# Keys and queries of a decoder layer's cross-attention by seven block products, with the context's keys from memory and two batches routed at a time

## The chip, the cores and the metric

The kernel runs on one core of a Trainium2 chip. The metric is the device time of one execution in microseconds, the median of the runs. All arithmetic is in 32-bit floats.

## The reference

Sixteen batches of 256 tokens of width 256 (`x`) pass a post-norm decoder layer of three parts; each batch has a context of 77 rows of width 256.

```python
x = layernorm(x + recurrence(x))
x = layernorm(x + cross_attention(ctx, x))
x = layernorm(x + experts(x))

# cross_attention, 8 heads of 128; xn, ln: normed context and tokens, with gains and biases
q = ln @ Wq + bq
kv_input = concatenate([xn, ln], axis=1)          # 77 + 256 rows
k, v = split(kv_input @ Wkv + bkv, 2)
attn = softmax((q * DH**-0.5) @ k.T)              # each head: 256 x 333
out = (attn @ v) @ Wo + bo

# experts: each token to its 2 best of 8 (512 wide), each expert takes its first 512 tokens
```

The recurrence is a projection to 512, a convolution over four tokens, silu, and a scan over the tokens with 16 states. What counts here is `k` and `q`: both are products of the same 256 tokens, K from 333 rows (the tokens and the context), Q from the 256 tokens alone.

## The kernel before, in words

**Stages.** A start loads weights and prepares batch 0. Then 128 heads (16 batches of 8) run one after the other, and between them, by a table written out by hand, the pieces of all other work: the recurrence of later batches, the preparation of the next batch's keys and values, the projection, norm, scoring and routing of the batch before. A stage for the experts follows.

**A head.** `head_kq` (L581) makes K of a head in two products with 333 moving columns (L587; 256 tokens and 77 context rows, `kvt`) and Q in two with 256 (L592); ACT moves both out of the accumulator with bias and scale (L589, L594). `head_softmax` makes the scores (L602) in one two-bank tile, DVE takes the row maximum (L604), ACT the exponentials with their sums (L608), DVE the reciprocal and the normed rows `pn` (L610, L613). `head_turn` transposes these on TensorE (L625); DVE copies the first 512 columns (`ptt`, L627) and ACT the 77 rows of the context (L628). `head_out` multiplies with the values (L639) and ACT moves the result out (L647). The loop (from L1263) interleaves three heads:

```python
        if i < len(heads):
            head_kq(*heads[i])
            for f, args in steps[heads[i]]:
                f(*args)
        if i >= 2:
            head_out(*heads[i - 2])
        if i < len(heads):
            head_softmax(*heads[i])
        if 1 <= i <= len(heads):
            turned = head_turn(*heads[i - 1])
        if i < len(heads):
            for f, args in late_steps[heads[i]]:
                f(*args)
```

`steps` and `late_steps` are the table: `at(b, h, ...)` puts a piece ahead of a head's output product, `behind(b, h, ...)` after the turn. A scheduler lays the instructions out on each engine's queue near this order; each queue then runs in order, SyncE's (SP) DMA queue too.

**Seven products.** Values and projection already use the scheme by which a product of two-by-two blocks takes seven block products in place of eight, with sums of blocks: `prep_values` (L541) with `tsum` (sums of token blocks, `prep_sums`, L530, on GpSimd) and `wsum`; `project_pairs` (L711, its products at L729) with 128-column products that each have their own weights. Keys and queries do not use it.

**Context.** `context_turn` (L431) turns the normed context into `kvc`, an SBUF tile for all batches; `context` (L454) makes the context's values once and stores them in memory (`vc`), from where each batch loads its rows (L549). The context's keys are computed again in every head, as 77 of the 333 columns.

**Routing.** `choose` (L838) finds each token's two experts by some sixteen small DVE operations on 128x16, `dispatch` (L880) counts places by two small products (L886, L887), computes the rows by some twenty more small DVE operations and scatters the tokens by four indirect DMAs of GpSimd (L921). Both run for each batch. What later stages must know of a token lies in six columns behind its 256 (`DX = D + 6`).

**Recurrence.** `rec_in` (L315) is a piece of projection and convolution: four passes of 512 columns on TensorE (L324), two ACT operations (L333, L342) and five DVE operations (L337, L339 three times, L344). `rec_state` (L348) ends with a product `pp` (L385) that waits for DVE's `zb`, and the scan.

Of the kernel before, what the change touches and what calls it, by code (L numbers as in the profile page):

```python
# [10 lines left out]
F32 = mybir.dt.float32  # L11
I32 = mybir.dt.int32
# [26 lines left out]
def decoder_layer(  # L39
# [40 lines left out]
    xpool = ctx.enter_context(tc.tile_pool(name="x", bufs=5))  # L80
# [11 lines left out]

    vc_d = dram.tile([B * M, INNER], F32, tag="vc", name="vc")
# [10 lines left out]
    rev = cpool.tile([P, GT, E], F32, tag="rev", name="rev")  # L104
    ebase = cpool.tile([P, GT, E], F32, tag="ebase", name="ebase")
# [79 lines left out]
    wosum = wpool.tile([P, 3, H // 2, P], F32, tag="wosum", name="wosum")  # L185
    wsum = wpool.tile([P, 4, 512], F32, tag="wsum", name="wsum")

    kvc = wpool.tile([P, DC, B * M], F32, tag="kvc", name="kvc")
# [40 lines left out]
    ctx_ends = [b2.tile([P, 1, D], F32, tag="ctx", name=f"ctx{t}") for t in (0, NCT - 1)]  # L229
# [55 lines left out]
    V.tensor_scalar(bqs, bq_s, DH**-0.5, None, ALU.mult)  # L285

# [61 lines left out]
    def rec_state(first, last):  # L348
# [34 lines left out]
        A.activation(dec[R], dec[R], AF.Exp, scale=-1.0)  # L383
        pp = bank(f"pp{first}")
        T.matmul(pp[R, 0:S], lhsT=perm[R, R], rhs=zb[R], start=True, stop=True)  # L385
        bs = aw.tile([P, S], F32, tag="bs", name=f"bs{first}")
# [42 lines left out]
    turns = {}  # L429

    def context_turn(t, first):  # L431
# [11 lines left out]
        for k in range(DC):  # L443
            T.transpose(pt[:, k * P : k * P + rows], zc[0:rows, 0, k * P : (k + 1) * P], ident[0:rows, 0:rows])
        for k in range(DC):
            A.activation(
                kvc[:, k, t * P : t * P + rows],
                pt[:, k * P : k * P + rows],
                AF.Identity,
                bias=bm[:, k : k + 1],  # L450
                scale=gm[:, k : k + 1],
            )

    def context(t, first):  # L454
# [4 lines left out]
        for half in range(2):  # L459
# [9 lines left out]
            for k in range(DC):  # L469
                T.matmul(  # L470
                    pv[0:rows],
                    lhsT=kvc[:, k, t * P : t * P + rows],
# [10 lines left out]
        if first:  # L483
            nc.sync.dma_start(vc_d[t * P : t * P + rows, :], stages[t // 2][0:rows, t % 2, :])

# [17 lines left out]
    def prep_keys(b):  # L503

        zl = zs.pop(b)
        kvt = b2.tile([P, DC, J], F32, tag="kvt", name=f"kvt{b}")
        G.tensor_copy(kvt[:, :, S:J], kvc[:, :, b * M : (b + 1) * M])
# [22 lines left out]
    def prep_sums(b):  # L530

        x = lambda i, k: kvts[b][:, k, i * P : (i + 1) * P]
        sums = b1.tile([P, 4, P], F32, tag="tsum", name=f"tsum{b}")
# [47 lines left out]
    def head_kq(b, h):  # L581

        kvt = kvts[b]
        f = slice(h * DH, (h + 1) * DH)
        pk = bank(f"pk{b}_{h}", "pk", 1)
        for k in range(DC):
            T.matmul(pk[:, 0:J], lhsT=wkv_s[:, k, f], rhs=kvt[:, k, :], start=(k == 0), stop=(k == DC - 1))  # L587
        kt = b2.tile([P, J], F32, tag="kt", name=f"kt{b}_{h}")
        A.activation(kt, pk[:, 0:J], AF.Identity, bias=bkv_s[:, h : h + 1])  # L589
        pq = bank(f"pq{b}_{h}", "pq", 1)  # L590
        for k in range(DC):
            T.matmul(pq[:, 0:S], lhsT=wq_s[:, k, f], rhs=kvt[:, k, 0:S], start=(k == 0), stop=(k == DC - 1))  # L592
        qt = b2.tile([P, S], F32, tag="qt", name=f"qt{b}_{h}")
        A.activation(qt, pq[:, 0:S], AF.Identity, bias=bqs[:, h : h + 1], scale=DH**-0.5)  # L594
        kts[b, h], qts[b, h] = kt, qt

    def head_softmax(b, h):
# [7 lines left out]
        p = b2.tile([P, 2, J], F32, tag="p", name=f"p{b}_{h}")  # L605
# [5 lines left out]
        pn = b2.tile([P, 2, J], F32, tag="pn", name=f"pn{b}_{h}")  # L611
        for ic in range(2):
            V.tensor_scalar(pn[:, ic, :], p[:, ic, :], rs[:, ic : ic + 1], None, ALU.mult)  # L613
        pns[b, h] = pn

    def head_turn(b, h):
# [10 lines left out]
        turned = V.tensor_copy(ptt[:, 0:2, :], pt01.rearrange("p (j i) -> p j i", j=2))  # L627
        A.copy(ptt[0:M, 2, :], pt2[0:M, 0:S])  # L628
        ptts[b, h] = ptt
        return turned  # L630
# [18 lines left out]
    pws, norms, xbs = {}, {}, {}  # L649
# [104 lines left out]
    def norm_half(b, i):  # L754

        if i == 0:
            xbs[b] = b1.tile([P, 2, D], F32, tag="xb", name=f"xb{b}")
# [4 lines left out]
        y = b2.tile([P, D], F32, tag="yl", name=f"yl{b}_{i}")  # L762
# [18 lines left out]
    def settle_now(b):  # L781
        r2 = again(*norms.pop(b), f"o{b}")
        o = b1.tile([P, 2, D], F32, tag="yb", name=f"o{b}")
# [29 lines left out]
    def score_experts(b):  # L813
# [12 lines left out]
        lgs[b] = small.tile([P, GT, E], F32, tag="lg", bufs=2, name=f"lg{b}")  # L826
        V.tensor_copy(lgs[b].rearrange("p t e -> p (t e)"), pl[:, 0 : GT * E])

    def t3(tag, b):
        return small.tile([P, GT, E], F32, tag=tag, bufs=2, name=f"{tag}_{b}")  # L830

    def t2(tag, b):
        return small.tile([P, GT], F32, tag=tag, bufs=2, name=f"{tag}_{b}")

    def wide(t):
        return t.unsqueeze(2).broadcast_to([P, GT, E])

    def choose(b):  # L838


        def first_max(src, k, km):
# [6 lines left out]
            V.tensor_tensor(key, eq, rev, ALU.mult)  # L848
            V.tensor_reduce(km, key, AX.X, ALU.max)
            oh = t3(f"oh{k}", b)  # L850
            V.tensor_tensor(oh, key, km.unsqueeze(2).broadcast_to([P, GT, E]), ALU.is_equal)
# [3 lines left out]
        x = xs[b]  # L855
        wa, wb, km1 = x[:, :, D], x[:, :, D + 1], x[:, :, D + 3]
        for i in range(GT):
            G.tensor_scalar(x[:, i, D + 2 : D + 3], tok1, float(b * S + i * P), 1.0, ALU.add, ALU.mult)
        lg = lgs.pop(b)
# [18 lines left out]
        chosen[b] = oh1, oh2m, on  # L878

    def dispatch(b):  # L880

        oh1, oh2m, on = chosen.pop(b)

        pc = bank(f"pc{b}")
        onf = on.rearrange("p t e -> p (t e)")
# [480 lines left out]
```

## Time and profile before

| | before |
|---|---|
| median of 3 runs, us | 1165.93 (1164.40 to 1166.26) |
| the profiled execution: its time, its span, us | 1174.61, 1172.9 |
| busy, us: PE, weight loads, DVE | 1140.7, 833.5, 812.1 |
| busy, us: ACT, GpSimd | 494.5, 321.2 |
| K products (L587), Q products (L592), scores (L602), us | 165.3, 131.2, 164.3 |
| row maximum (L604), turn's copy on DVE (L627), us | 108.3, 87.2 |
| granted TensorE clock | 0.998 |

PE is TensorE, DVE VectorE, ACT ScalarE, POOL GpSimd, SP SyncE. "Busy" is the union of an engine's instructions; those of PE are pipelined, so a row's length is more than its share of the time. A group's row gives busy time, the mean of one in ns, and the idle time of the engine ahead of it with what ended most of it. A row of the waits view is the waiting instruction, what it waited for, total us, times, and the longest.

### The profile page before, as it was taken

How to read it: one execution, taken by the hardware profiler on the slowest of the kernel's cores; microseconds unless marked ns; L12 is line 12 of the kernel's file. 1: busy time of each engine (PE TensorE's matmuls, PEld its weight loads, DVE VectorE, ACT ScalarE, POOL GpSimd, SP SyncE). 2: the span in 40 equal slices, each digit the busy share in tenths (PEclk: the TensorE clock that was granted, in tenths of full speed). 3: DMA queues.
4: the chain of work that ended last, by engine and by line, in shares of the span. 5: the costliest groups of instructions: out<-in, count | busy, mean ns of one | idle time of the engine just before them, and what ended most of it. 6: DMA issues, size and time to landing. Idle time of an engine off the chain costs nothing. (4 is left out here: it accounts for less than half of the span.)

```text
span 1172.9 us, 16419 instructions
## 1 busy us (share of the span) xinstructions
PE 1140.7 (97%) x5436; PEld 833.5 (71%) x5436; DVE 812.1 (69%) x2367; ACT 494.5 (42%) x1298; POOL 321.2 (27%) x564
## 2 busy tenths in 40 slices
PE   7999999999999999999999999999999999999996
PEld 3465676777787877677777777687877778876664
DVE  6655878686757776876678767766576664665665
ACT  3344444443444444444445444444444443523331
POOL 2211243113311331232213322232122212144454
PEclk9999999999999999999999999999999999999999
DMA  7740101001000010000000100000001000045752
GB/s 253 217 144 33 35 22 37 12 28 39 24 25 17 28 37 22 27 29 19 15 10 24 37 14 10 14 19 14 10 14 46 24 10 12 21 162 137 180 161 87
DMA packets 47149, 60.67 MB, mean 52 GB/s; under 512 B 7941, under 2 KB 37102, under 8 KB 47064
## 3 DMA queue, kind: packets, MB, share of 16 engines
q1 hardware_dynamic: 39686, 50.31, 13.5%
q0 software_dynamic: 6048, 9.22, 3.1%
q8 instruction: 43, 0.70, 0.3%
q14 instruction: 42, 0.34, 0.1%
q10 hardware_dynamic: 1330, 0.10, 0.1%
HBM read 36.33 MB, written 30.78 MB: 57 GB/s over the span
## 5 line engine op out<-in xcount | busy, mean ns | idle before, releaser
L639 PE MATMUL po<-ptt,v 128*128 128x256 f32 (+1 forms) x768 | 190.9, 382 | 1.6 <-DVE rs L610 1.6
L639 PEld LDWEIGHTS po<-ptt,v 128*128 128x128 f32 (+1 forms) x768 | 141.5, 190 | 53.1 <-issue 35.5
L587 PE MATMUL pk<-kvt,wkv_s 128*128 128x333 f32 x512 | 165.3, 444 | 0.0
L602 PE MATMUL s<-kt,qt 128*128 128x333 f32 x512 | 164.3, 442 | 0.0
L604 DVE TENSOR_REDUCE nm<-s 128x2 f32<-128x666 f32 x128 | 108.3, 846 | 54.3 <-PE s L602 54.1
L608 ACT ACTIVATE p<-s,nm 128x333 f32<-128x333 f32 x256 | 135.4, 535 | 22.6 <-DVE nm L604 21.9
L647 ACT ACTIVATE ot<-po,bkv_s 128x256 f32<-128x256 f32 x128 | 60.8, 475 | 172.0 <-PE po L639 171.0
L592 PE MATMUL pq<-kvt,wq_s 128*128 128x256 f32 x512 | 131.2, 379 | 0.0
L587 PEld LDWEIGHTS pk<-kvt,wkv_s 128*128 128x128 f32 x512 | 91.1, 191 | 45.9 <-issue 23.2
L602 PEld LDWEIGHTS s<-kt,qt 128*128 128x128 f32 x512 | 96.5, 189 | 30.9 <-issue 0.5
L592 PEld LDWEIGHTS pq<-kvt,wq_s 128*128 128x128 f32 x512 | 96.7, 189 | 30.5 <-issue 0.5
L628 ACT COPY ptt<-pb 77x256 f32<-77x256 f32 x128 | 47.2, 369 | 163.1 <-PE pb L625 163.1
L613 DVE TENSOR_SCALAR pn<-p,rs 128x333 f32<-128x333 f32 x256 | 100.8, 429 | 3.3
L921 POOL DMA_INDIRECT xg<-xs,sidx x64 | 65.6, 1025 | 89.2 <-DVE sidx L918 58.5
L627 DVE COPY ptt<-pa 128x512 f32<-128x512 f32 x128 | 87.2, 682 | 0.6 <-PE pa L625 0.6
L625 PEld LDWEIGHTS pa<-ident,pn 128*128 128x128 f32 x512 | 63.9, 141 | 29.3
L589 ACT ACTIVATE kt<-pk,bkv_s 128x333 f32<-128x333 f32 x128 | 68.9, 538 | 24.6 <-PE pk L587 23.8
L625 PE MATMUL pa<-ident,pn 128*128 128x128 f32 x512 | 76.8, 273 | 0.0
L339 DVE SCALAR_TENSOR_TENSOR cv<-hp,cw,cv 128x512 f32<-128x512 f32 (+1 forms) x108 | 73.9, 691 | 1.4
L594 ACT ACTIVATE qt<-pq,bqs 128x256 f32<-128x256 f32 x128 | 61.0, 477 | 18.8 <-PE pq L592 14.9
L324 PE MATMUL ph<-xT,inw 128*128 128x512 f32 (+1 forms) x144 | 63.4, 570 | 5.0 <-DMA inw<-in_in_wT 4.9
L1183 PE MATMUL pf<-w,it 128*128 128x256 f32 x272 | 61.3, 381 | 2.7 <-ACT ye L1193 1.5
(254 smaller groups left out, 1826.8 us busy)
## 6 DMA issues: line engine op xcount, KB each, us to landing
v<-vc SPq DMA_DIRECT2D x16, 308.0 KB
xg<-zero SPq DMA_DIRECT2D x34, 131.0 KB
xe<-xg SPq DMA_DIRECT2D x8, 524.0 KB
xt<-in_x_in SPq DMA_DIRECT2D x16, 256.0 KB
out<-o SPq DMA_DIRECT2D x16, 256.0 KB
w<-in_w1T SPq DMA_DIRECT2D x8, 512.0 KB
w<-in_w2T SPq DMA_DIRECT2D x8, 512.0 KB
oe<-ye SPq DMA_DIRECT2D x15, 256.0 KB
```

Of the source, the lines that this page charges most:

```text
L339: V.scalar_tensor_tensor(cv, hp[:, :, k : k + S], cw[:, c, k : k + 1], cv, ALU.mult, ALU.add)
L587: T.matmul(pk[:, 0:J], lhsT=wkv_s[:, k, f], rhs=kvt[:, k, :], start=(k == 0), stop=(k == DC - 1))
L589: A.activation(kt, pk[:, 0:J], AF.Identity, bias=bkv_s[:, h : h + 1])
L592: T.matmul(pq[:, 0:S], lhsT=wq_s[:, k, f], rhs=kvt[:, k, 0:S], start=(k == 0), stop=(k == DC - 1))
L602: T.matmul(s[:, ic, 0:J], lhsT=qt[:, ic * P : (ic + 1) * P], rhs=kt, start=True, stop=True)
L604: V.tensor_reduce(nm, s[:, :, 0:J], AX.X, ALU.max, negate=True)
L608: A.activation(p[:, ic, :], s[:, ic, 0:J], AF.Exp, bias=nm[:, ic : ic + 1], accum_out=sm[:, ic : ic + 1])
L613: V.tensor_scalar(pn[:, ic, :], p[:, ic, :], rs[:, ic : ic + 1], None, ALU.mult)
L625: T.transpose(dst[0:jn, c0 : c0 + P], pn[:, ic, j0 : j0 + jn], ident)
L627: turned = V.tensor_copy(ptt[:, 0:2, :], pt01.rearrange("p (j i) -> p j i", j=2))
L639: T.matmul(po[:, 0:S], lhsT=vs[b][0:jn, jc, h * DH : (h + 1) * DH], rhs=ptt[0:jn, jc, :], start=(jc == 0), stop=(jc == 2),)
L921: dma = G.indirect_dma_start(out=xg[:, :], out_offset=bass.IndirectOffsetOnAxis(ap=sidx[:, t, c : c + 1], axis=0), in_=xs[b][:, t, :], in_ ...
```

## The change

Keys and queries of a head become one product of two-by-two blocks (token halves by channel halves; K and Q side by side), in seven 128-column products in one bank, `kq_first` three and `kq_second` four; the sums of the tokens are the ones that the values already use. Their combination is one ACT copy, one ACT operation and five DVE operations of 128 columns. Batch 0 still uses plain products, with the context's columns left out, since its weight sums (`kq_weights`, DVE) are made during it, partly in the place of `wq_s`; so the scale of the queries is put into the weights ahead (`scale_queries`, ACT). The context's keys are computed once (`context_keys`), stored in memory (`kc`), and loaded by a DMA in each head. The products of a head are issued one head ahead. The normed rows are written in place; the turn's copy of 512 columns goes from DVE to ACT. `rec_state` is cut before `pp`: `rec_scan` runs behind the output product. `choose` and `dispatch` run once for two batches (on 128x32, eight scatters in a row, with an ACT copy of the six columns ahead), except for the last two batches. Pools are re-cut to make room.

```diff
+    def scale_queries():
+        A.activation(wq_s..., wq_s..., AF.Copy, scale=DH**-0.5)
...
+    def context_keys(t, first):
+        rows = ctx_rows(t)
...
+            for h in range(4):
+                f = half * 512 + h * DH
+                for k in range(DC):
+                    T.matmul(
+                        pk[:, h, 0:rows],
+                        lhsT=wkv_s[:, k, f : f + DH],
+                        rhs=kvcs[t][:, k, 0:rows],
...
+            bias = bkv_s[:, heads].unsqueeze(2).broadcast_to([P, 4, rows])
+            V.tensor_tensor(kc[:, :, 0:rows], pk[:, :, 0:rows], bias, ALU.add)
+            nc.sync.dma_start(kc_d[:, heads, t * P : t * P + rows], kc[:, :, 0:rows])
...
+    def kq_weights(h):
+        f = slice(h * DH, (h + 1) * DH)
+        t = lambda i: kqsum[:, i, h - BLOCKS[0], :]
+        V.tensor_tensor(t(0), wq_s[:, 0, f], wkv_s[:, 0, f], ALU.subtract)
+        V.tensor_tensor(wq_s[:, 0, f], wq_s[:, 1, f], wq_s[:, 0, f], ALU.subtract)
+        V.tensor_tensor(t(1), wq_s[:, 1, f], t(0), ALU.subtract)
+        V.tensor_tensor(t(2), wkv_s[:, 1, f], t(1), ALU.subtract)
...
+    def kq_first(b, h):
...
+        nc.sync.dma_start(kt[:, S:J], kc_d[:, h, b * M : (b + 1) * M])
...
+        kq_product(b, h, ((0, 1), (1, 5), (2, 7)), True)
+        parts_kq[b, h] = u = b2.tile([P, 3, P], F32, tag="ukq", bufs=1, name=f"ukq{b}_{h}")
+        A.copy(u.rearrange("p r d -> p (r d)"), pk[:, 0 : 3 * P])
+        V.scalar_tensor_tensor(u[:, 1, :], u[:, 1, :], bqs[:, h : h + 1], u[:, 2, :], ALU.add, ALU.add)
+
+    def kq_second(b, h):
...
+        kq_product(b, h, ((3, 6), (0, 2), (2, 4), (1, 3)), False)
...
+        A.activation(kt[:, 0:P], pk[:, 0:P], AF.Identity, bias=bkv_s[:, h : h + 1])
+        u0 = u[:, 0, :]
+        V.tensor_tensor(u0, u0, pk[:, 3 * P :], ALU.add)
+        V.scalar_tensor_tensor(kt[:, P:S], pk[:, 2 * P : 3 * P], bkv_s[:, h : h + 1], u0, ALU.add, ALU.add)
+        V.scalar_tensor_tensor(qt[:, 0:P], pk[:, P : 2 * P], bqs[:, h : h + 1], u0, ALU.add, ALU.add)
+        V.tensor_tensor(qt[:, P:S], u0, u[:, 1, :], ALU.add)
...
-        turned = V.tensor_copy(ptt[:, 0:2, :], pt01.rearrange("p (j i) -> p j i", j=2))
+        A.copy(ptt[:, 0:2, :], pt01.rearrange("p (j i) -> p j i", j=2))
...
-            at(b, 6 - early, choose, b - 1)
-            at(b, 7 - early, dispatch, b - 1)
+            if b == B - 1:
+                at(b, 6 - early, choose, b - 1, 1)
+                at(b, 7 - early, dispatch, b - 1, 1)
+            elif b % 2 == 0:
+                at(b, 6, choose, b - 2, 2)
+                at(b, 7, dispatch, b - 2, 2)
...
+        if i + 1 < len(heads):
+            kq_first(*heads[i + 1])
         if i < len(heads):
-            head_kq(*heads[i])
             for f, args in steps[heads[i]]:
                 f(*args)
         if i >= 2:
             head_out(*heads[i - 2])
         if i < len(heads):
-            head_softmax(*heads[i])
+            for f, args in mid_steps[heads[i]]:
+                f(*args)
+        if i + 1 < len(heads):
+            kq_second(*heads[i + 1])
+        if i < len(heads):
+            turned = head_softmax(*heads[i])
         if 1 <= i <= len(heads):
-            turned = head_turn(*heads[i - 1])
+            head_turn(*heads[i - 1])
```

## The prediction

> **What bounds the kernel now.** I read the page first: the busy times, then the forty slices.
>
> ```profile
> PE 1140.7 (97%) x5436; PEld 833.5 (71%) x5436; DVE 812.1 (69%) x2367; ACT 494.5 (42%) x1298; POOL 321.2 (27%) x564
> ...
> PE   7999999999999999999999999999999999999996
> ...
> DVE  6655878686757776876678767766576664665665
> ```
>
> PE is busy in every slice but the first and the last; DVE, the next engine, is at six to eight tenths. A busy PE need not be a packed one, so next I took the windows view for one batch in the middle (about 62 us) and the first batch.
>
> ```profile
> 43.00:120.00 77.00, 75.09 (x276) 44.87 (x276) 47.45 (x105) 33.89 (x88) 7.45 (x20) 1.00 0.37 109
> 616.00:678.00 62.00, 62.00 (x310) 46.96 (x309) 49.30 (x139) 28.37 (x75) 21.83 (x41) 1.00 0.10 29
> ```
>
> The columns are the stretch, PE, weight loads, DVE, ACT, POOL, granted clock, DMA share and GB/s. PE has no gap in the batch. The timeline of PE alone says whether it is packed: what counts there is the distance from one start to the next, since a row's own length holds the pipeline's tail.
>
> ```profile
> 524.01 1.28 PE L602 MATMUL s<-kt,qt 128*128 128x333 f32 x4
> 525.13 0.60 PE L625 MATMUL pa<-ident,pn 128*128 128x128 f32 x4
> 525.78 1.29 PE L587 MATMUL pk<-kvt,wkv_s 128*128 128x333 f32 x4
> 526.91 1.02 PE L592 MATMUL pq<-kvt,wq_s 128*128 128x256 f32 x4
> 527.77 1.05 PE L729 MATMUL pw<-wosum,ot 128*128 128x128 f32 x8
> 528.66 1.06 PE L729 MATMUL pw<-wo_s,ot 128*128 128x128 f32 x8
> ```
>
> An f32 product is two passes. Four passes of 333 columns take 525.78 to 526.91 = 1.13 us (0.282 each), four of 256 take 0.86 (0.215), eight of 128 take 0.89 (0.112; the next sixteen the same); per column 0.85, 0.84 and 0.87 ns. PE streams columns end to end, and nobody makes it wait. So **columns removed are time removed, until another engine becomes late.** The heads are where that must be read: scores 1.12, turn 0.65 (six transposes), K and Q 1.99, output 1.30 (six passes of 0.215) give 5.06 us for a bare head, and the batch's other work is spread among the heads.
>
> **PE's work, term by term.** (1) K and Q of a head: before 1.13 + 0.86 = 1.99; after, in batches 1 to 15, seven products of two passes of 128: 14 x 0.112 = 1.57. Gain 0.42 x 120 = **50**. (2) In batch 0, K and Q without the context: eight passes of 256, 1.72; gain 0.27 x 8 = **2**. (3) The context's keys are not saved, only moved: nine tiles of 128 rows with 32 passes each, 9 x 32 x 0.112 = 32.3, and one of 80 rows, about 2.3 (32 passes at 0.07, by columns). Cost **35**: half in the start, half in batch 0. (4) Routing in pairs: the two counting products (four passes at 0.11) are issued seven times less: gain **3**. PE's sum: 50 + 2 + 3 - 35 = **-20**.
>
> The price of a 128-column pass decides the sign. The row L729 is the nearest case: each pass with its own weights, 0.112 us over 32 in a row. At the 256-column price per column it would be 0.108 (another 7 us of gain); 0.116 would take 7 away. The Trainium skill speaks against narrow products ("TensorE: Matmul & The Clock Gate", Back-to-back issue gap): sustained, 128 columns cost about 81 ns a matmul where the columns alone need 56, since the weight load counts too. By that ratio term (1) would be a loss of some 0.2 us a head. The row above does not show it.
>
> **The split of the recurrence.** The waits view of PE has this:
>
> ```profile
> PE pp L385 <- issue: 3.9, 3, 1.3
> ```
>
> Three times PE stands 1.3 us before `pp`, with part of the output product behind it. Now the whole output product (1.30) lies in front. Between 0 and 4 gained; I take **-3**.
>
> **DVE, the term I trust least.** These are the rows of the groups by form:
>
> ```profile
> L604 DVE TENSOR_REDUCE nm<-s 128x2 f32<-128x666 f32 x128 | 108.3, 846 | 54.3 <-PE s L602 54.1
> L613 DVE TENSOR_SCALAR pn<-p,rs 128x333 f32<-128x333 f32 x256 | 100.8, 429 | 3.3
> L627 DVE COPY ptt<-pa 128x512 f32<-128x512 f32 x128 | 87.2, 682 | 0.6 <-PE pa L625 0.6
> L339 DVE SCALAR_TENSOR_TENSOR cv<-hp,cw,cv 128x512 f32<-128x512 f32 x84 | 63.2, 753 | 1.3
> L743 DVE TENSOR_TENSOR xb<-xb,u 128x128 f32<-128x128 f32 x28 | 8.1, 290 | 5.4 <-ACT u L741 5.0
> ```
>
> Before, a head costs DVE 0.85 + 0.16 (reciprocal) + about 0.75 (two `pn`, overlapping) + 0.68 = 2.4 us. After, the copy of 0.68 goes to ACT and five operations of 128 columns come, at 0.29 like L743: 1.76 + 1.45 = 3.2. That is +0.77 x 120 = 92 us; the pairing of routing (some 35 small operations of 0.12 to 0.17, seven times less) gives back about 33, and the additions of the context's bias and the weight differences cost 14 + 9. DVE's total becomes near 895 of a shorter span, some 78%: no bound on average. But it is lumpy. A piece of the recurrence (`rec_in`) costs DVE 0.55 + 3 x 0.75 + 0.69 = 3.5 us and PE four passes of 512, 1.72. With it a head is 4.64 + 1.72 = 6.4 for PE and 6.7 for DVE. The worst head holds a piece, scores, the choice and a value product: PE 4.64 + 1.72 + 0.45 + 0.86 = 7.7; DVE 3.2 + 3.5 + 0.7 + 2.2 = 9.6. Before it was 8.1 against 8.8, and PE did not wait.
>
> How much lateness is free? The next head's scores reuse the same bank, so PE waits once the row maximum is later than the head's length minus (1.12 + 0.2 + 0.85 + 1.15 for the two exponentials) = 3.3 us: 1.7 us free in a head of 5.0, 3 us in one of 6.4. By the built order of the instructions, counted row by row, DVE has more work than PE in about 16 heads: heads 5 of batches 2, 6, 10 (2 each), 6 of batches 4, 8 (2), head 0 of seven odd batches (about 2), some smaller: **30 us of excess**. Carrying it along by hand through batch 6, PE is late by 0.9 at head 3 (the turn's copy is behind a tanh that waits for DVE) and 1.8 at head 6: near 3 us. Three such batches 8, batches 4/5 and 8/9 about 3 in all, batch 1 about 2: **+13**, bounds 4 (slack absorbs nearly all) and 30 (none).
>
> **ACT and the turn.** ACT loses K and Q (0.54 + 0.48) and gets a copy of 384 columns (0.48 by L741), 128 columns of K (about 0.36) and the turn's copy of 512 (0.58 by L571): +0.4 a head, 47 us in all, ACT near half busy. But the turn's two copies now run one after the other, 0.58 + 0.37: from the end of the turn's products about 1.15 us until the output product may start, where only the next head's first three products (0.67) are sure to cover it. Bare, that is a wait of 0.45. Nearly every head has other work there (value products 0.86, the projection 2.7 to 3.6, routing, transposes); without that cover it would be 0.45 x 120 = 54. I take 0 beyond the +13, whose bound holds it.
>
> **The keys from memory.** A DMA of 39 KB a head is issued by SP when the buffer's last reader, scores two heads earlier, is done, and K's writers wait for it: about 3.5 us in a bare head, 5 to 6 in most. For its landing the nearest transfer is `v<-vc`, 308 KB, issued at 516.42:
>
> ```profile
> 517.00:518.00 1.00, 1.00 (x9) 0.84 (x8) 1.00 (x5) 0.00 (x0) 0.00 (x0) 1.00 0.50 111
> 518.00:519.00 1.00, 1.00 (x6) 0.72 (x5) 0.90 (x4) 0.43 (x2) 0.76 (x2) 1.00 0.60 221
> 519.00:520.00 1.00, 1.00 (x6) 0.81 (x5) 1.00 (x2) 1.00 (x5) 1.00 (x2) 1.00 0.00 0
> ```
>
> It has moved by 519, at most 2.6 us after its issue; the small one needs no more. So it is hidden, if SP is free. SP is not: in its order stand loads and stores that wait for others.
>
> ```profile
> SPq L549 <- PE po L639: 384.3, 13, 40.6
> SPq L786 <- POOL o L785: 379.0, 16, 46.4
> ```
>
> In the built order each `out` is put just after the key load of the head in which POOL should have finished it, so most of that wait (46 us was idle time, with nothing behind it) should vanish. If POOL is late, K's rows are, then ACT's queue with the turn behind them, and PE. I take 0; the bound is 2.5 us a batch for 15 batches, 38. The Trainium skill ("DMA: Bandwidth & Descriptors", Specifications) says that pieces under 512 B do not run at line rate, and a row of keys is 308 B. No run so far shows what that costs this transfer; by the page's fixed 2 us and twice the time for 39 KB it would be an estimate of 2.2 us.
>
> **Start and end.** In the first 43 us PE is idle 7.7, of which 4.9 is the first load. The new products may fill up to 2.8, and the scaling of the query weights on ACT (2048 columns, about 1.9 us by L571's slope) and 14 more us of DVE work may cost as much: 0. The last routing has an ACT copy before its scatter, 0.2: 0. The experts are unchanged.
>
> **Sum:** -20 - 3 + 13 = **-10 us** on the profiled execution, 1174.61 us (span 1172.9, the rest around it). That one is 0.7% above the median of the runs, 1165.93; the same amount off the median gives **1156**.
>
> **Rivals.** *Clean pass*: DVE's excess fits in the slack, all waits at their low ends: -20 - 4 + 4 = -20, and 7 more if a pass costs 0.108: 1139 to 1148, say 1145. For it: PE waits for nothing now at 69% DVE. Against: the 9.6 against 7.7. *Nothing left*: the waits eat the sum: 1166. *Slower, DVE becomes the bound in the heads with recurrence and routing*: all 30 of excess is paid, and the turn's copy is late by 0.45 in the 28 heads with a piece of the recurrence (13): -23 + 43 = +20, 1186; it decides from 23 us of waiting, 0.19 us a head, and its middle is near 1174. For it: the free time in a bare head is only 1.7 us and two in-order queues pass work back and forth four times a head. Against: seven of sixteen batches have no piece, and there DVE is at 82% or less. *Slower, late keys*: +38 - 10 = 1194. *It does not do what it says*, PE's passes cost more than 0.112 between waits: 0.15 a pass would be 14 x 0.038 x 120 = 64, about 1220; L729 speaks against it.
>
> **Chances.** Forecast 1156 (own range 1148 to 1163): 0.42. Clean: 0.20. Nothing left: 0.10. DVE bound: 0.20. Late keys 0.06, dear passes 0.02. So faster by over 0.2% (what a measurement of this kernel can tell from no change) 0.62, within 0.10, slower 0.28. The range 1140 to 1178 leaves out the late keys, the upper part of the DVE rival and the lowest end of the clean one.
>
> **What will show it.** Passes of `pk` 0.112 apart: term (1). A first batch and start together some 30 to 35 us longer, later batches 2.5 to 3.4 us shorter: the trade of (3) for (1). Waits of PE at `s` and `pa` for DVE or ACT, in heads with a piece of the recurrence: the +13. `ptt` released by ACT's own queue: the turn. Waits on the key load in ACT or DVE: the late keys. It is wrong if PE waits in heads without a piece, or if batch 12 to 14, with almost no DVE load, do not gain 3 us each.

## The result, and the profile after

| | before | after |
|---|---|---|
| median of 13 runs each, us | 1165.93 (1164.18 to 1166.82) | 1168.48 (1165.00 to 1169.60) |
| ratio, 95% interval | | 1.0024 (1.0016 to 1.0032) |
| profiled execution: time, span, us | 1174.61, 1172.9 | 1169.54, 1167.8 |

The forecast was 1156, faster; the change made the kernel 2.5 us slower. The two profiled executions alone say the opposite, 5.1 us faster. That contradiction was the first thing to settle. The page of after:

```profile
PE 1135.0 (97%) x6448; PEld 878.1 (75%) x6448; DVE 862.2 (74%) x2674; ACT 539.2 (46%) x1436; POOL 312.5 (27%) x548
...
PE   7999999999999999999999999999999999999996
...
DVE  6764578879877887888669878886777676656765
```

PE is still busy everywhere; DVE is now at eight or nine tenths in many slices. The windows of the same two stretches (columns as before):

```profile
43.00:120.00 77.00, 75.74 (x371) 51.80 (x371) 42.24 (x104) 25.32 (x63) 7.18 (x18) 1.00 0.54 156
616.00:678.00 62.00, 60.11 (x359) 47.48 (x358) 53.44 (x166) 31.33 (x86) 24.13 (x42) 1.00 0.12 33
```

The times are the same and not the work: after is about 11 us behind there (batch 9 starts at 637.8 us, before at 626.4). The middle stretch held no gap of PE before; now 1.9 us of it are empty, and GpSimd (POOL) has 24 us. The timeline of PE in a head without a wait:

```profile
912.43 0.39 PE L641 MATMUL pk<-tsum,kqsum 128*128 128x128 f32 x2
912.65 0.39 PE L641 MATMUL pk<-kvt,wkv_s 128*128 128x128 f32 x2
912.88 0.39 PE L641 MATMUL pk<-kvt,kqsum 128*128 128x128 f32 x2
913.10 0.39 PE L641 MATMUL pk<-tsum,wq_s 128*128 128x128 f32 x2
913.32 1.29 PE L694 MATMUL s<-kt,qt 128*128 128x333 f32 x4
```

Eight passes take 912.43 to 913.32 = 0.89 us: 0.111 each. Over all 1680 passes of L641 the median distance is 0.112, the price of the forecast. The groups by form of the engines beside PE:

```profile
L696 DVE TENSOR_REDUCE nm<-s 128x2 f32<-128x666 f32 x128 | 108.2, 845 | 2.2 <-PE s L694 2.1
...
L685 DVE SCALAR_TENSOR_TENSOR kt<-pk,bkv_s,ukq 128x128 f32<-128x128 f32 x120 | 41.5, 346 | 1.7
```

```profile
L719 ACT COPY ptt<-pa 128x512 f32<-128x512 f32 x128 | 74.9, 585 | 140.5 <-PE pa L717 140.5
```

The idle time ahead of the row maximum `nm` fell from 54.3 to 2.2 us: DVE hardly waits for the scores now, it comes to them late. The five added operations are 0.28 to 0.36 us long (estimated 0.29), but their starts are 0.20 to 0.31 us apart, since rows overlap; DVE's total is 862.2 us and not the 895 of the forecast. The turn's copy on ACT waits for PE's transposes and nothing else. PE's own waits:

```profile
PE pe L1266 <- DMA xe<-xg: 4.1, 2, 2.1
PE s L694 <- ACT p L700: 3.4, 12, 1.0
...
PE pw L820 <- DVE osum L795: 2.4, 2, 1.2
```

No wait on the key load is among them: the rival of the late keys did not come.

**Where the time went.** The start of the scores of each batch cuts the span into stages. Before is taken from a second profile of it (first experiment below), whose execution is typical:

| stage, us | before | after | difference | forecast | last version below |
|---|---|---|---|---|---|
| start to the first scores | 52.6 | 70.2 | +17.6 | } +33 | 69.6 |
| batch 0 | 82.6 | 98.1 | +15.5 | } | 98.1 |
| batches 1 to 15, to the last scores | 878.5 | 845.2 | -33.3 | -43 | 835.8 |
| last scores to the end | 151.3 | 154.4 | +3.1 | 0 | 154.2 |
| span | 1165.0 | 1167.8 | +2.8 | -10 | 1157.8 |

By batch, 1 to 15: -5.9, -1.0, -2.2, -2.9, -0.4, -2.0, -2.1, -2.9, -0.3, -2.0, -2.1, -2.9, -1.9, -2.6, -2.0. Batches 5 and 9 gained nearly nothing, 3, 7, 11 and 13 less than 12.

**A measure of waits.** Idle time hides part of a wait, as a row's length holds the pipeline's tail. So I also summed, over all passes of PE, the distance to the next start less the median of that shape: in batches 1 to 15 it is 5.5 us in before (second profile) and 24.2 in after. The new waits are 18.7 us.

### The profile page after: what moved, and what is told of

The parts are those of the page before. It is cut to its first block, busy times and chain, and to the rows that moved or that the text cites. A ratio compares the mean times of both kernels' runs of the same rounds, so it can differ in the third digit from the quotient of the medians.

```text
span 1167.8 us, 19269 instructions
## 1 busy us (share of the span) xinstructions
PE 1135.0 (97%) x6448; PEld 878.1 (75%) x6448; DVE 862.2 (74%) x2674; ACT 539.2 (46%) x1436; POOL 312.5 (27%) x548
## 3 DMA queue, kind: packets, MB, share of 16 engines
q1 hardware_dynamic: 68678, 60.41, 17.2%
## 5 line engine op out<-in xcount | busy, mean ns | idle before, releaser
L719 ACT COPY ptt<-pa 128x512 f32<-128x512 f32 x128 | 74.9, 585 | 140.5 <-PE pa L717 140.5
L704 DVE TENSOR_SCALAR p<-p,rs 128x333 f32<-128x333 f32 x256 | 94.8, 412 | 3.3
L641 PE MATMUL pk<-tsum,kqsum 128*128 128x128 f32 x480 | 94.2, 277 | 2.1 <-ACT ukq L670 1.9
L641 PE MATMUL pk<-tsum,wq_s 128*128 128x128 f32 x480 | 92.8, 275 | 0.0
L641 PE MATMUL pk<-kvt,wkv_s 128*128 128x128 f32 x480 | 92.7, 275 | 0.0
L641 PEld LDWEIGHTS pk<-kvt,wkv_s 128*128 128x128 f32 x480 | 76.1, 191 | 21.4 <-issue 21.0
L641 PEld LDWEIGHTS pk<-tsum,kqsum 128*128 128x128 f32 x480 | 80.0, 190 | 14.6 <-ACT ukq L670 8.0
L717 PEld LDWEIGHTS pa<-ident,p 128*128 128x128 f32 x512 | 63.6, 141 | 29.2 <-DVE p L704 0.6
L717 PE MATMUL pa<-ident,p 128*128 128x128 f32 x512 | 77.0, 273 | 0.0
L641 PEld LDWEIGHTS pk<-tsum,wq_s 128*128 128x128 f32 x480 | 72.9, 192 | 0.0
L670 ACT COPY ukq<-pk 128x384 f32<-128x384 f32 x120 | 57.7, 481 | 29.5 <-DVE qt L687 24.6
```

The source lines that it names most:

```text
L641: T.matmul(pks[b, h][:, r * P : (r + 1) * P], lhsT=w[n - 1], rhs=tsums[b][n - 1], start=first and r == 0, stop=True, skip_group_check=True,)
L704: ends = V.tensor_scalar(p[:, ic, :], p[:, ic, :], rs[:, ic : ic + 1], None, ALU.mult)
L717: T.transpose(dst[0:jn, c0 : c0 + P], pn[:, ic, j0 : j0 + jn], ident)
L719: A.copy(ptt[:, 0:2, :], pt01.rearrange("p (j i) -> p j i", j=2))
```

## The experiments

Each set of kernels ran on one chip beside before. In the first set (k1 to k4) and the fifth (k16 to k18) before took 1167.0, in the other three 1174.4 to 1174.8; so a kernel is compared by its ratio to before of its own set. Stage and batch times, and PE's waits by head, are read from the one profiled execution of each kernel.

### Before once more (k1_before)

No edit. 

> The kernel before, unchanged, for a second profile. The pair of profiled executions says that the change takes 5.1 us off (1174.61 to 1169.54), the medians say that it adds 2.5 (1165.93 to 1168.48): the profiled execution of before is 8.7 us above its own median, that of after 1.1. Theory A, the yardstick was bad: the new profile has a span near 1164 us, and the 8.7 us lie in stages that the change does not touch (the start, the experts); then the forecast's terms stand. Theory B, the terms were bad: the 8.7 us lie in batches 1 to 15, so that a true batch of before is about 0.5 us shorter than the first profile showed, and the gain of a batch by the change 2.1 and not 2.6 us. Third possibility: a profile of before is 8 us too long every time.

Median 1166.43 (ratio 0.9993, 0.9984 to 1.0003), span 1165.0. So the first profile was not typical. It is 7.9 us longer, in two places: batches 2, 6 and 10 are 66.1 to 66.2 there and 64.6 here (4.8 us), and the experts' stage 155.3 against 151.3 (the start is 1.2 us shorter there). Theory A had the span right; of the place each theory had half. The timeline of DVE, first profile of before:

```profile
266.77 0.48 DVE L380 TENSOR_SCALAR zb<-px,xpb 128x256 f32<-128x256 f32 x1 [2.62 <-PE po L639]
```

and the second:

```profile
266.13 0.48 DVE L380 TENSOR_SCALAR zb<-px,xpb 128x256 f32<-128x256 f32 x1 [0.84 <-PE px L360]
```

The product `px` before it had started at 262.98 and at 264.12: `zb` came 3.79 us behind it in the one, 2.01 in the other. In the first, PE stood 1.3 us before `pp` for that `zb`; in the second, not at all. The -3 of the forecast was the price of this stall.

### Plain products (k2_plain)

```diff
-        if b == 0 or h not in BLOCKS:
+        if True:
...
-        behind(0, min(h, H - 2), kq_weights, h)
```

> The changed kernel with plain products of 256 columns for keys and queries in all batches (eight passes of 0.215 = 1.72 us a head against 14 x 0.112 = 1.57), no weight sums, all else kept. If TensorE's passes decide: 0.15 x 120 = 18 us slower than after, 1186. If the lateness of VectorE and ScalarE eats the gain of the seven products: VectorE loses five operations of 128 columns a head (1.45 us), waits shrink by up to 13 us, and the time is 1173 to 1178.

1207.53, 1.0350 of before. Both numbers were too low. The span is 39.3 above after's; 20.7 of it are waits in batches 1 to 15 (44.9 by the measure above, against 24.2), among them a new one:

```profile
PE pk L665 <- ACT kt L663: 6.3, 9, 1.6
```

The plain products of a head stand all ahead of the output product, so nothing covers the second half, and Q's products wait until ACT has read K from the same bank. The other 18.6 us agree with the price of the columns (0.15 x 120 = 18).

### Routing unpaired (k3_unpaired)

```diff
-        first, i = (b, 0) if b >= B - 2 else (b - b % 2, b % 2)
+        first, i = b, 0
...
+            at(b, 6 - early, choose, b - 1, 1)
+            at(b, 7 - early, dispatch, b - 1, 1)
```

> The changed kernel with each batch routed by itself, at the heads where before had it. Forecast terms: TensorE +3 us; VectorE +33 us of small operations, in heads that are already its fullest. If VectorE has slack enough: 1171. If its lumps set the time: 1178 to 1190.

1174.16, 1.0067. Pairing is worth about 5 us (1.0067 less 1.0024 of 1167), nearer to the first number. In batches 1 to 15 it is 5.5: 3 of PE and 2.4 of waits (26.6).

### The turn's copy on DVE (k4_turndve)

```diff
-        A.copy(ptt[:, 0:2, :], pt01.rearrange("p (j i) -> p j i", j=2))
+        V.tensor_copy(ptt[:, 0:2, :], pt01.rearrange("p (j i) -> p j i", j=2))
```

> The changed kernel with the turn's copy of 512 columns on VectorE again (0.68 us) and not on ScalarE (0.585). If VectorE is the late engine in the full heads: 82 us more work on it (81% of the span busy) cost 10 to 30 us: 1178 to 1198. If ScalarE's queue with its two copies in a row is what TensorE waits for: 3 to 6 us faster than after, 1163 to 1165.

1214.73, 1.0405: worse than the worst number. DVE is busy 934 us, 77% of the span, and waits rise to 68.5 us, with PE's longest

```profile
PE s L694 <- issue: 19.6, 5, 6.2
```

in batches 3, 5, 7, 9 and 11. So DVE bounds this kernel long before it is busy all the time. That the work which two or three heads in a row hold decides is a reading of where the waits stand, not shown apart.

### What DVE is late for: four single edits

The timeline of DVE in after, batch 13, head 3, a batch without any piece of the recurrence:

```profile
888.96 0.25 DVE L684 TENSOR_TENSOR ukq<-ukq,pk 128x128 f32<-128x128 f32 x1
889.70 0.74 DVE L151 TENSOR_SCALAR xs<-xb,mvb,rb 128x256 f32<-128x256 f32 x2 [0.49 <-POOL rb L137]
890.35 0.16 DVE L148 TENSOR_SCALAR va<-mva 128x2 f32<-128x2 f32 x1
890.42 0.35 DVE L685 SCALAR_TENSOR_TENSOR kt<-pk,bkv_s,ukq 128x128 f32<-128x128 f32 x1
891.32 0.77 DVE L151 TENSOR_SCALAR xs<-xt,mva,ra 128x256 f32<-128x256 f32 x2 [0.56 <-POOL ra L137]
892.01 0.34 DVE L686 SCALAR_TENSOR_TENSOR qt<-pk,bqs,ukq 128x128 f32<-128x128 f32 x1
892.26 0.28 DVE L687 TENSOR_TENSOR qt<-ukq 128x128 f32<-128x128 f32 x1
892.46 0.84 DVE L696 TENSOR_REDUCE nm<-s 128x2 f32<-128x666 f32 x1
```

The scores of this head ended at 888.84 and K's products at 887.7, but the row maximum starts at 892.46. Between them stand the combination of K and Q, and between its operations two layer norms that wait for a root computed on GpSimd. DVE's queue is served in order, so what waits there for GpSimd delays the next head's keys, its scores, and PE.

**The recurrence joined again (k5_recjoin):** `rec_scan(first)` is called at the end of `rec_state`. 

> The changed kernel with the recurrence not split: the product pp follows its zb at once, ahead of the output product, as in before. The forecast priced the split at a gain of 3 us, from three waits of 1.3 us before pp in the first profile of before. In the second profile of before these waits are not there (the row starts 0.22 us after the one ahead of it). If the stall belongs to the kernel: 3 us slower than after, 1171.5. If it belonged to that one execution: within 1 us of after, 1167.5 to 1169.5.

1183.29, 1.0087 (1.0052 to 1.0121); after in the next set was 1.0056 (1.0035 to 1.0076). The median is above after's by what the first theory said, but the intervals overlap, and the profile has the difference elsewhere (the end is 160.3 us, 156.9 in after's second profile). Batches 6 and 10, where the two parts meet, are 62.54 in both, and `zb` starts 0.06 us behind the end of `px` in both. The split gained nothing there: the forecast's term is not there to be gained.

**One operation of the combination left out (k6_less):** the line `V.scalar_tensor_tensor(u[:, 1, :], ...)` is deleted. 

> The changed kernel without one of the five VectorE operations of the combination, u1 + u2 + bias, 0.34 us a head in batches 1 to 15 (a part of the queries lacks one product and the bias; all else runs as before). If the 19 us of TensorE's waits that after has more than before come from VectorE being late in full heads: 41 us less work on it take 6 to 12 us off, 1156 to 1162. If ScalarE's queue or the order of issue makes them: within 2 us of after.

1188.93, 1.0136: slower by some 9 us, which neither theory allows. Batches 5, 9, 13 and 15 lost 1.7, 4.7, 1.5 and 3.4 us against after's second profile (k9_after below). The scheduler laid the queues out anew (on PE, ACT and DVE the order is no longer that of after), and PE waits 7.6 us for the projection's inputs from DVE (`ot`, 0.8 in after). As a price of DVE's work it says nothing.

**The norms behind the turn (k7_norm):**

```diff
+    def project_norm(b):
+        norms[b] = layernorm(xs[b], xbs[b], 2, P, f"b{b}")
...
+                behind(b, 3, project_norm, b - 1)
...
-            at(b, 3, rec_out, nb + 1)
+            behind(b, 3, rec_out, nb + 1)
```

> The changed kernel with two layer norms (of the projection, and of the pair's second batch) put behind the turn of head 3 and not ahead of its output product. In after, in odd batches, the four VectorE operations that make K and Q stand behind these norms, which twice wait about 0.5 us for GpSimd; the row maximum of head 3 starts 3.6 us after its scores have ended, and TensorE waits 0.5 us for it in each of six odd batches, 0.7 and more in batch 13. If this queue is what is late: 3 to 4 us faster than after, 1164.5 to 1165.5. If the lateness only moves on to the next head: no change within 1 us.

1176.39, 1.0023 (1.0004 to 1.0042), so 3.9 us below after's 1.0056: the size that the first theory named, though the two intervals overlap. The measure of waits, taken head by head, shows the place: head 3 of batches 3, 5, 7, 9, 11 and 13 holds 0.62 to 0.63 us of PE's waits in after and none here, 3.7 us in all. (Batch 5 has 4.3 us more in head 1 in this execution.)

**A piece of the recurrence moved (k8_rec4):** `(0, 5), (0, 7), (1, 0), (1, 5)` becomes `(0, 4), (0, 5), (0, 7), (1, 5)`. 

> The changed kernel with one piece of the recurrence moved from head 0 of batches 5 and 9 to head 4 of batches 4 and 8. These two batches gained 0.3 us each where the other odd ones gained 2: eight scatters, twenty small VectorE operations of two batches' routing and that piece meet there, and the projection waits 1.3 us for VectorE's sums. If that meeting is the cause: 3 to 6 us faster than after, 1162.5 to 1165.5. If head 4 of the even batches, the shortest for TensorE (5.50 us), is late instead: no change or up to 2 us slower.

1188.64, 1.0128. Batches 4 and 8 became 1.2 us shorter each, 5 and 9 6.5 to 6.7 longer. The timeline of GpSimd and of DVE in batch 5 shows why:

```profile
412.41 0.97 POOL L1021 DMA_INDIRECT xg<-xs,sidx  x1 [0.30 <-issue]
413.69 0.97 POOL L1021 DMA_INDIRECT xg<-xs,sidx  x1 [0.31 <-issue]
414.67 1.29 POOL L351 TENSOR_TENSOR sums<-sums,hs 128x512 f32<-128x512 f32 x1
...
417.13 0.72 POOL L137 TENSOR_TENSOR ra<-va,nhalf 128x2 f32<-128x2 f32 x1
...
417.88 1.46 DVE L151 TENSOR_SCALAR xs<-xt,mva,ra 128x256 f32<-128x256 f32 x2 [4.17 <-POOL ra L137]
```

Eight scatters in a row, 1.3 us apart, hold GpSimd from 404.1 to 414.7; behind them stands the root `ra`, for which DVE waits 4.17 us with the projection's input `ot` behind it, for which PE waits 4.4. Pairing the routing made this row of eight. The waits of DVE in before (second profile):

```profile
DVE xs L150 <- POOL ra L136: 4.1, 10, 0.8
...
DVE zl L500 <- POOL rlz L136: 3.2, 6, 0.5
DVE xs L150 <- POOL rb L136: 1.8, 5, 0.8
...
DVE zl L496 <- POOL rlz L136: 1.3, 1, 1.3
```

and in after:

```profile
DVE xs L151 <- POOL ra L137: 13.8, 16, 2.0
...
DVE xs L151 <- POOL rb L137: 6.7, 15, 0.8
...
DVE zl L539 <- POOL rlz L137: 0.9, 1, 0.9
```

From 5.9 to 20.5 us for `ra` and `rb`; with `rlz`, for which before waits 4.5 and after 0.9, from 10.4 to 21.4. Most of that is not the scatters' doing: without them (k16_noscatter below) it is still 17.1. The forecast had no term for GpSimd's roots.

### GpSimd's order

**After once more (k9_after):** no edit. 

> The changed kernel, unchanged, once more beside before, as the yardstick for the other kernels of this set. In the last set before itself took 1174.8 us, 8 more than in the two sets ahead of it, so its numbers are read against each other only. If the change is worth the same wherever it runs: 1.0016 to 1.0032 of before. If the late release after products of 32 rows or columns, seen in the first profile of before (VectorE's zb 1.8 us after px had ended) and in the last set (xt 2.0 us after py), costs the two kernels differently: outside that.

1180.60, 1.0056 (1.0035 to 1.0076): the interval does not touch the first one. The change is worth less in these sets. Against after in the table above, batches 3, 7, 11 and 13 are 1.5 to 2.0 us longer each, in head 1, and the experts' stage 2.6; the others agree to 0.2. The late release is there:

```profile
531.95 1.56 PE L730 MATMUL po<-ptt,v 128*128 128x256 f32 x6
...
534.75 0.97 POOL L1021 DMA_INDIRECT xg<-xs,sidx  x1 [0.30 <-issue]
...
537.08 0.47 ACT L738 ACTIVATE ot<-po,bkv_s 128x256 f32<-128x256 f32 x1 [4.24 <-PE pa L717]
```

`po` ends near 533.5, and ACT, idle since 532.8, copies it at 537.08 only.

**Scatters split (k10_scatter):** four of the eight go behind the turn of head 1 of the next batch, issued after `ra`. 

> The changed kernel, in which four of the eight scatters of a pair are issued behind the root ra of the norm in head 1 of the next batch, and not all eight ahead of it. Theory: GpSimd's eight scatters in a row (1.3 us each) hold up the roots ra and rb; VectorE's queue waits for them 20.5 us in after against 5.9 in before, and behind that wait stand the four operations that make K and Q and the sums of the projection. If so: 1 us less in each of batches 3, 7, 11, 13, 2 to 3 us in 5 and 9, so 6 to 9 us faster than after in the same set. If GpSimd's order does not matter: within 1.5 us of it.

1190.53, 1.0128: 10 us slower than k9_after, not 6 to 9 faster. The wait moved to the next root:

```profile
DVE zl L543 <- POOL rlz L137: 14.8, 6, 5.0
```

In after `rlz` costs 0.9. That GpSimd's order matters is shown by this miss; it suggests a place for the scatters behind the last root of a batch.

**The clock (k11_fill):**

```diff
+            if t == 0:
+                for _ in range(20):
+                    T.transpose(pt[:, 0:P], ident, ident)
```

and 16 such transposes in the experts' stage. 

> The changed kernel with 20 more transposes of the identity ahead of the first turn of the context and 16 ahead of the turn of the third block of tokens of the experts, where TensorE waits 2.57 and 2.14 us and the granted clock then falls to 0.5 for 3.3 us. The added products do nothing for the output. If the low clock costs what it takes away, half of 3.3 us twice: up to 3.3 us faster than after in the same set. If both stretches wait for memory in any case: within 1 us, or slower by what the fill itself takes.

1183.13, 1.0076 (1.0064 to 1.0089), not faster than k9_after. The granted clock is 1.00 through both places, the first scores come 0.8 us earlier, the experts' stage is 0.3 us longer. So the up to 3.3 us of the first case are not there. That both stretches wait for loads in any case fits the DMA share of 1.00 to 1.05 in them, but is not shown apart.

**Split scatters and late norms (k12_both):** 

> The scatters as in the kernel with the split scatters, and the two layer norms of head 3 behind the turn (as in the kernel tried alone). If the in-order wait of VectorE for GpSimd's roots is what makes TensorE late in the odd batches: 8 to 12 us faster than after in the same set, and so 5 to 9 us faster than before. If the norms only move the lateness: as with the scatters alone, within 1.5 us.

1177.10, 1.0034 (1.0021 to 1.0047): 3.5 us below k9_after and not 8 to 12, about what the norms alone gave. Against the split scatters alone the norms are worth 13.4 us, so the second case is out too.

**All scatters late (k13_late8):**

```diff
+    def scatter_late(b):
+        if b + 5 in normed:
+            with tc.issue_after(normed[b + 5].ins):
+                scatter(b, 2)
...
+                at(b + 1, 4, scatter_late, b - 2)
```

> The changed kernel with all eight scatters of a pair put into head 4 of the odd batch, behind that batch's last root of a norm, where GpSimd has nothing that VectorE waits for soon. Splitting the scatters moved VectorE's wait from ra (13.8 us to 9.6) to rlz (0.9 to 14.8, six times, 5.0 at most), and was 10 us slower: what stands behind the scatters on GpSimd decides. If that is the cause of the waits in the odd batches: VectorE waits for ra, rb and rlz together about 16 us (21.4 in after), batches 3, 5, 7, 9, 11, 13 gain 1 to 3 us each, and the time is 6 to 10 us below after, 0.996 to 0.999 of before. If the scatters are not the cause: 1.0024 to 1.0056 of before, as after was.

1180.98, 1.0061: no gain. DVE's waits for `ra`, `rb` and `rlz` are 17.1 us together, as expected, but in k9_after they were 17.2 already, so this count does not tell the two apart. Batches 3, 7, 11 and 13 gained 0.9 to 1.3 against k9_after: their wait in head 1 is gone and another came in head 5. 5 and 9 lost 3.1 to 3.2 each: head 0 rose from 0.2 us of waits to 2.0, where DVE has a piece of the recurrence (3.5 us); whether that piece is the cause is tried in k18 below.

**Late scatters and norms (k14_late8norm)**, then with **two buffers (k15_late8normu)**, `tag="ukq", bufs=2`: 

> The late scatters, and the two layer norms of head 3 behind the turn. If the four operations that make K and Q stand behind the norms' wait for GpSimd's roots (0.5 us of TensorE in head 3 of each odd batch): 3 us below the kernel with late scatters alone. If it only moves the wait: the same within 1 us.

1177.59, 1.0028 (1.0010 to 1.0046), 3.4 us below k13_late8, as expected. 

> The same as the last, with two buffers for the copy of the first three products (ScalarE's copy waits for VectorE's last reading of the buffer; TensorE's second four products wait for that copy, 1.9 us in after, 7.5 in the kernel with split scatters and late norms). If VectorE's late operations reach TensorE by this buffer: 2 to 4 us below the kernel before it. If they reach it by the scores alone: the same within 1 us.

1183.21, 1.0075: slower. PE's wait for the buffer fell from 2.7 us to 0.6, and the waits for the turn's copies (7.9 to 8.9 us) and the projection's sums (2.0 to 4.4) grew. The buffer is not the cause.

### Leaving the scatters out (k16_noscatter, k17_before_noscatter)

`for t in range(TT)` becomes `for t in range(TT if b == B - 1 else 0)`, in before likewise. 

> The changed kernel without the scatters of batches 0 to 14 (60 of 64 left out: the experts then read cleared rows, all else is computed). Two claims. First, the late releases: in the last three sets ScalarE's copy of the output product started up to 3.9 us after the product, and only while a scatter was running (at most 0.04 us late in some 75 others of each kernel); without scatters none should be late. Second, the eight scatters in a row hold up GpSimd's roots. If both are the change's missing term: 9 to 12 us below after in a set like the last three (after 1180.6), 4 to 6 below it in a set like the first (1168.5), and at or below before without scatters. If the lateness comes from VectorE's added work alone: 0 to 3 us below after.

> The kernel before without the same 60 scatters, as the other half of the pair. Its first profile had zb late by 1.8 us in three places, 4.9 us of batches 2, 6 and 10, each beside four scatters. If scatters do that: 4 to 6 us below before in a set like the last three, 0 to 2 in a set like the first. The pair gives the change without scatters: by the stage tables of the first set (33.1 up at the start and batch 0, 33.2 down in batches 1 to 15, of which 6 to 9 of waits on GpSimd), 3 to 8 us faster.

1171.00 (1.0035) and 1171.66 (1.0039): both slower than with the scatters, and the pair's ratio is 0.9994. Both expectations missed: no gain of 4 to 6 us, and a change worth 0.7 us without scatters and not 3 to 8. As a leave-out of one cost it failed: the experts' stage, which now reads cleared rows, is 3.3 us longer in the one and 4.4 in the other, and I can't say why (before had 155.3 there in its first profile, with all scatters). In batches 1 to 15 the changed kernel gains 0.7 us, the size of the second case (0 to 3), and before 0.1. But the small sum hides an exchange, the same as in k13_late8: batches 3, 7, 11 and 13 gain 0.7 to 1.2 each, nearly all of it in head 1 (PE's waits there 0.55 to 1.10 us in after, none here), and 5 and 9 lose 1.6 to 1.7 each, in head 0 (waits from 0.24 to 2.06). So the scatters are one of two lumps, and taking one away uncovers the other. Late releases can't be judged here, since in this set the kernels with scatters have none either.

### Both lumps away (k18_late8normrec)

Late scatters, late norms, and the moved piece of k8_rec4. 

> The changed kernel with the late scatters, the late norms and the recurrence's piece of batches 5 and 9 moved to head 4 of the batch ahead. With the scatters late, batches 5 and 9 were 1.7 to 3.1 us longer than in after, in head 0, where that piece (3.5 us of VectorE) stands; moving it alone had made batches 4 and 8 1.2 us shorter, but let the scatters delay the root ra by 4.2 us in batches 5 and 9. If those are the two causes: 6 to 9 us below the kernel with late scatters and norms (1.0028 of before), 0.995 to 0.998 of before. If the lateness only moves on: the same as that kernel within 2 us.

1159.11 against 1167.01, **0.9936 (0.9921 to 0.9950)**: faster than both kernels, a little more than expected. (After has no run in this set; its 1.0024 is from sets in which before took as long as here.) Against after, batches 3, 7 and 11 gain 1.4 to 1.5 us, 13 2.0, 4 and 8 1.2 and 0.9, 5 and 9 0.2 and 0.3; PE's waits in batches 1 to 15 are 14.8 us (24.2 in after). Of its waits view for PE and DVE:

```profile
PE s L694 <- ACT p L700: 1.0, 1, 1.0
...
DVE xs L151 <- POOL ra L137: 5.5, 9, 0.8
```

The wait at the scores, twelve times in after, is left once (so it is with late norms and late scatters alone, k14_late8norm). By head, PE's waits in heads 1 and 3 of batches 3, 7, 11 and 13 are gone, and in head 0 of 5 and 9 they are 0.08 us (2.0 with late scatters and norms alone): the moved piece was that second lump. The same move had cost 8 us where the scatters stood ahead of it.

## Why the prediction was wrong, point by point

- **K and Q, term (1): right.** A pass is 0.112 us; plain products in its place cost 18 us of columns. What the Trainium skill says of narrow products ("TensorE: Matmul & The Clock Gate", Back-to-back issue gap) would have made a loss of it, by the prediction's estimate; 0.112 us for 128 columns beside 0.215 for 256 does not show it.
- **The context's keys, term (3): right.** Start and batch 0 together are 33.1 us longer (-2 + 35 foretold). So PE's sum of -20 stands, and nothing of the loss is in it.
- **The split of the recurrence, -3: wrong.** It was read from three rows that one execution had and the next had not. The same execution had 4 us more in the experts' stage. The step that failed is to take a row marked "issue", which named no cause, for a property of the kernel, and to move the difference of two executions of the same program unchanged to the median.
- **Waits, +13: mis-sized and misplaced.** 18.7 us, inside the bounds of 4 and 30. Foretold were 8 in batches 2, 6 and 10 (measured 4.2), 3 in 4, 5, 8 and 9 (7.5), 2 in batch 1 (-1.7), none elsewhere (8.7, of which 6.7 in 3, 7, 11 and 13). The prediction named its own test: wrong if PE waits in heads without a piece of the recurrence, or if batches 12 to 14 do not gain 3 each. They gained 2.9, 1.9 and 2.6, and PE waits in heads 1 and 3 of the odd batches. The failed step is to count DVE's load head by head and to leave out what DVE waits for: GpSimd's roots behind eight scatters, and two norms in front of the combination; POOL's queue was not walked. The load itself was counted too high (895 us, measured 862.2). The runs show the missing part by head: in batches 3, 7, 11 and 13 the wait in head 1 goes with the scatters, that in head 3 with the norms, and with both moved 6.3 of the 6.7 us are gone. In k18 9.4 of the 18.7 us are gone. Of the other 9.3, 4.2 stand in 2, 6 and 10 and 4.8 in 4, 5, 8 and 9, the batches to which the prediction had given its waits; the two runs that take load from DVE (k2_plain, k6_less) change too much else to say what makes them.
- **The turn on ACT, 0: right.** PE waits 1.1 us for it in all; on DVE it costs about 45.
- **Late keys, 0: right.** Nobody waits for a key load. It lands 1.7 us after its issue (median of 128); the prediction's estimate from a page's figures was 2.2.
- **Start and end, 0:** the start is in the 33.1. The end is 3.1 us longer, 2.2 of it before the first transposes of the experts, which wait for their rows 2.0 us (1.7 in k9_after and k18; in before's profiles not at all). The failed step is to call the experts unchanged and to price only an ACT copy of 0.2 us ahead of the scatters: those of batch 14 start 7.2 us before the last scores in after and 9.1 in before. What of this difference is routing that has got slower and what is heads that have got shorter stays open. The other 0.9 is less than what two profiles of before differ by in this stage (4.0). The clock is not the reason.

Together: 3 (split), 5.7 (waits) and 3.1 (end) of the 12.8 us between -10 and +2.8; the remaining 1 is the columns of batches 1 to 15, which by the same measure come to 52 us and not 53 (33.3 + 18.7). Of the 55 us that PE saves in the heads and in routing, 35 went back at the start and in batch 0, as foretold; the waits of a DVE queue that had got longer and stands behind GpSimd's made the rest a small loss. The outcome lies next to the rival "nothing left" (1166), to which the prediction had given one chance in ten.

## What to carry to other kernels

Take a stall from a profile into a sum only when a second profile of the same kernel has it too, above all when its releaser is "issue". Where an in-order engine gets new work, list not only its load but what each of its waiting instructions waits for, and what stands ahead of that on the third engine; here roots on GpSimd, some of them behind a row of scatters, decided in the odd batches when VectorE could go on, and so when TensorE did. Lumps that cover each other must be taken away together: two of the three edits alone gave nothing or a loss, the third (the norms) 3.9 us, all three made the kernel 0.6% faster than before. Whether two of them would do was tried for scatters and norms only (1.0028).

## What the runs showed of the hardware

- **Low clock after short gaps.** In the profiles of this study the granted clock fell to 0.5, for 3.4 us or twice that, after 44 of the 58 idle gaps of PE from 2.0 us on (not after one of 3.35), and after five shorter ones (0.9 to 1.9 us). The wait of 4.9 us ahead of PE's first product is not counted; no fall follows it in any profile. In after, gap (1047.2 to 1049.3) and fall:

```profile
1048.00:1049.00 1.00, 0.00 (x0) 0.00 (x0) 0.09 (x1) 0.00 (x0) 0.98 (x2) 1.00 1.00 302
1049.00:1050.00 1.00, 0.67 (x6) 0.68 (x7) 0.51 (x2) 0.00 (x0) 0.46 (x1) 1.00 1.05 281
...
1051.00:1052.00 1.00, 1.00 (x4) 0.79 (x3) 1.00 (x13) 0.04 (x1) 0.69 (x2) 0.50 1.10 392
```

  The Trainium skill ("TensorE: Matmul & The Clock Gate", HAM oscillation) gives the rule as no idle gaps over about 3.4 us; here most gaps from 2.0 us on were enough, and the measurement decides.
- **Late releases beside scatters.** In sets two to four (eleven kernels) ACT's copy of the output product, where ACT stood idle for it, started over 0.5 us (up to 3.9) behind the product's end in 52 of 112 cases with a scatter of GpSimd running, and in none of 873 without (there 0.04 at most). In the profiles of sets one and five and in the first of before it was never late, with or without. What differs between the sets is not shown (sets one and three are recorded with the same chip number, and only the second of these has it); the scatters go with it, but that they cause it was not tried where it occurs.
